# Softmax sums of four units in six: column blocks summed on VectorE and joined by a small product, in place of a product with ones

## The chip, the core and the metric

The kernel runs on one core of one Trainium2 chip. The metric is the time of one execution on the device in microseconds (us); a version's time is the median of its runs. The engines are TensorE (PE, with its weight loads shown apart as PEld), VectorE (DVE), ScalarE (ACT), GpSimd (POOL) and SyncE (SP), which issues most transfers. [...]

## The reference

Input x is 8 images of 384 channels and 32x32 pixels in float32. Four layers follow one another, each as x = x + layer(groupnorm(x)). Layer 0 is an attention with depthwise convolutions ahead of its projections, layer 1 a mixture of four experts, layer 2 a quantized depthwise and pointwise convolution, and layer 3 a deformable attention. Only layer 3's attention is touched:

```
q  = einsum(x, q_w)                       # 6 heads of 64 channels, 1024 queries
kv = einsum(x_s, kv_w)                    # x_s: 256 sampled positions
attn = softmax(q . k * 64**-0.5)          # over the 256 keys
out  = proj_w . (attn . v) + proj_b
```

The softmax needs, for each head and each query, the sum of 256 exponentials.

## The kernel before

Layer 0 is computed for all images first, up to about 1630 us. Then the images go through layers 1 to 3 one behind the other: a generator `layers(b)` records layers 2 and 3 of image b, and between its steps the main loop records units of layer 1 of image b+1 (three products each: `hidden`, tile ph, or `result`, tile y) so that TensorE has work while others are waited for. Each `yield` of the generator states how much time TensorE is expected to have free; when the sum reaches `UNIT` (2.6), a unit of layer 1 is recorded. The instruction order on each engine is then set by a scheduler, which may move an instruction ahead of one that was recorded before it, and tiles come from pools whose buffers are used again in turn.

Layer 3's attention of an image is `attend`. It has six units: three pairs of heads (`pr`), each in two halves of 512 queries (`h`). The two heads of a pair lie side by side: in the columns of scores and exponentials (2 x 512), and in the two halves of 64 partitions of what comes out. A unit u is made so:

- `scores`: the products of keys with queries, for the two halves of the keys (kc = 0, 1), into two tiles s of 128 keys x 1024.
- `exps`: ACT takes the exponential of each, tiles p, in SBUF. They come from the pool `flat`, which has five buffers and also serves `p01` and, at the start of the next image's layer 1, the three tiles `o` that are loaded from HBM.
- POOL adds the two halves: p01 = p[0] + p[1], 128 partitions x 1024.
- `weigh`: values times exponentials, tile pav, 64 partitions for each head x 512 queries. PSUM's pool for pav (`ps_v`) has one bank.
- `sums` (L1899): a product of ones (128x64) with p01, for each head 512 columns, so that every one of the 64 partitions of a head holds the sums of its 512 queries (tile pss, from the pool `ps_f` of three banks, which ph and y also use).
- DVE transposes pav in 32x32 blocks into tu (L1935), and in `divide` pss in the same way into ts (L1907); in ts the sum of a query is the same along 32 columns, so one column of each block is enough: a reciprocal of 128x16 (L1909), a multiply of tu (L1910), and a transpose back into att (L1913).

A matrix product in float32 is made of two passes on TensorE. The products of `weigh` and `sums` for the two heads use the two halves of the array's columns.

The loop is shifted by one: in the round of unit u, the scores of unit u+1 are recorded ahead of `weigh` for unit u, and the sums and the division are those of unit u-1 (`due3`). The last unit's sums and division follow the loop, then the projection (tile pf).

The reciprocals are also kept in `rec3`; at the end of the program their range is looked at, and if one is out of range, layer 3 is done again in a general way.

Of the kernel before, what the change touches and what calls it, by code (L numbers as in the profile page):

```python
# [7 lines left out]
F32 = mybir.dt.float32  # L8
AF = mybir.ActivationFunctionType
ALU = mybir.AluOpType  # L10
AX = mybir.AxisListType

B, C, H, W = 8, 384, 32, 32
N = H * W
P = 128
# [20 lines left out]
NPAIR3, HS, LS, NG = 3, 16, 256, 3  # L36
# [19 lines left out]
def tile_kernel(ctx: ExitStack, tc: tile.TileContext, i: dict, out: bass.AP):  # L56
    nc = tc.nc
# [3 lines left out]
    small = ctx.enter_context(tc.tile_pool(name="small", bufs=2))  # L61
# [205 lines left out]
    with ExitStack() as pa:  # L267
# [254 lines left out]
        for n, (u, kind, s) in enumerate(work):  # L522
            k, h = divmod(u, 2)
# [29 lines left out]
            if kind == "v":  # L553
                h, c = h + s, 0
# [5 lines left out]
            for p in passes:  # L560
                j, x = p
                c0, c1 = max(0, 1 - x), W - max(0, x - 1)
                for q in range(nq):
# [3 lines left out]
                    elif kind == "y":  # L567
                        g, j, w = s, q, slice(0, 64)
# [4 lines left out]
                    for r, rs in enumerate(quads):  # L573
                        nc.tensor.matmul(  # L574
                            banks[r][cols[q]].rearrange("p (h w) -> p h w", w=W)[:, :, c0:c1],
                            lhsT=cws[rs, c, 2 * h + g, x, w],
                            rhs=src[rs, :, c0 + x - 1 : c1 + x - 1],
                            start=(p == passes[0]), stop=(p == passes[-1]),
# [13 lines left out]
            for q in range(4):  # L592
                rows = quads[q]
                if kind == "y":
                    v, j = divmod(q, 2)
# [5 lines left out]
                else:  # L601
                    g, j = divmod(q, 2)
# [69 lines left out]
    with ExitStack() as pb:  # L672
# [252 lines left out]
        for k in range(2):  # L925
            qs = slice(k * HALF // 2, (k + 1) * HALF // 2)
            for m in range(KC):
                for c in range(KC):
                    nc.tensor.matmul(
                        pos[m][:, qs], lhsT=wo0[:, c, m * P : (m + 1) * P],  # L930
                        rhs=atts[B - 1][:, c, HALF:][:, qs], start=(c == 0), stop=(c == KC - 1),
# [24 lines left out]
    _, sco, sho = sc_o  # L956
# [51 lines left out]
    with tc.If(redo > 0):  # L1008
        with ExitStack() as pb:
# [5 lines left out]
            for v, nm in enumerate(("wq0", "wk0", "wv0")):  # L1015
                t = wb.tile(list(i[nm].shape), F32, name=f"{nm}_e")
# [6 lines left out]
            with tc.For_i(0, B) as bi:  # L1023
# [11 lines left out]
                for t in range(NT8):  # L1035
                    pv = bank(f"pv_e{t}")
                    for c in range(KC):
                        nc.tensor.matmul(
                            pv[:, :C], lhsT=act[2][:, c, t * P : (t + 1) * P],
                            rhs=w_in[2][:, c, :], start=(c == 0), stop=(c == KC - 1),  # L1040
# [8 lines left out]
                for v in range(2):  # L1049
                    ts = qp.tile([P, NPAIR0, N], F32, tag=f"qk{v}", name=f"qk{v}_e")  # L1050
                    for pr in range(KC):
                        for h in range(2):
                            pq = bank(f"pq{v}_e{pr}_{h}")
                            for c in range(KC):
                                nc.tensor.matmul(
                                    pq, lhsT=w_in[v][:, c, pr * P : (pr + 1) * P],
                                    rhs=rows_of(act[v][:, c, :], h * H // 2, (h + 1) * H // 2) if v == 0
                                    else act[v][:, c, h * HALF : (h + 1) * HALF],
                                    start=(c == 0), stop=(c == KC - 1),
# [8 lines left out]
                for pr in range(NPAIR0):  # L1068
                    qt, kt = qks[0][:, pr, :], qks[1][:, pr, :]
                    for h in range(2):  # L1070
                        pav = bank(f"pav_e{pr}_{h}")
                        for j, r in enumerate(HR):
                            hd = 2 * pr + j
                            pt = qp.tile([P, NT8, HALF], F32, tag="pt", name=f"pt_e{pr}_{h}_{j}")
                            for qc in range(4):
# [3 lines left out]
                                for kh in range(2):  # L1079
# [3 lines left out]
                                        start=True, stop=True,  # L1083
# [3 lines left out]
                                p = pp.tile([P, N], F32, tag="p", name=f"p{nm}")  # L1087
# [14 lines left out]
                            for kc in range(NT8):  # L1102
                                nc.tensor.matmul(
                                    pav[64 * j : 64 * j + 64, :],
                                    lhsT=vt[:, kc, 2 * hd : 2 * hd + 2, :].rearrange(
                                        "p a b -> p (a b)"
                                    ),
                                    rhs=pt[:, kc, :],
# [38 lines left out]
    def load_w(name):  # L1147
        src = i[name]
        t = wd.tile(list(src.shape), F32, tag=name, name=name + "_sb")
        nc.sync.dma_start(out=t, in_=src)  # L1150
        return t
# [237 lines left out]

    x2_dram = dram.tile([B, P, KC, N], F32, name="x2")  # L1390
    om_dram = dram.tile([B, 3, NG * LS], F32, name="omd")
    NU3 = 2 * NPAIR3
    rec3 = wd.tile([P, B * NU3, 16], F32, name="rec3")
    bad3 = wd.tile([P, 1], mybir.dt.int32, name="bad3")

# [428 lines left out]
    def attend(pl, b, xt, put, general, q, xs, fill=nothing):  # L1824
# [69 lines left out]
        if not general:  # L1894
            def sums(u, p01):

                pss = fbank(f"pss3_{b}_{u}")
                for j in range(2):
                    nc.tensor.matmul(  # L1899
                        pss[64 * j : 64 * j + 64, :], lhsT=ones[:, :64],  # L1900
                        rhs=p01[:, j * HALF : (j + 1) * HALF], start=True, stop=True,
                    )
                return pss

            def divide(pss, pr, h, u, tu):
                tss = pl.one([P, 16, 32], "ts", f"ts_{b}_{u}")
                nc.vector.transpose(tss.rearrange("p a b -> p (a b)"), pss)  # L1907
                rc = rec3[:, b * NU3 + u, :]
                nc.vector.reciprocal(rc, tss[:, :, 0])  # L1909
                nc.vector.tensor_tensor(  # L1910
                    tu, tu, rc.unsqueeze(2).to_broadcast([P, 16, 32]), ALU.mult
                )
                nc.vector.transpose(  # L1913
                    att[:, pr, h * HALF : (h + 1) * HALF], tu.rearrange("p a b -> p (a b)")
                )


            ps, due3 = exps(0, scores(*units[0])), None
            fill(1)
            yield UNIT  # L1920
            for u, (pr, h) in enumerate(units):
                p01 = pl.flat([P, N], f"p01_{b}_{u}")
                nc.gpsimd.tensor_tensor(p01, ps[0], ps[1], ALU.add)  # L1923
                nxt = scores(*units[u + 1]) if u + 1 < NU3 else None
                if last and nxt:
                    nxt = exps(u + 1, nxt)
                pav = weigh(pr, h, ps)
                if due3:
                    pss = sums(due3[2], due3[4])
                if nxt:  # L1930
                    ps = nxt if last else exps(u + 1, nxt)

                tu = pl.one([P, NG * LS], f"om{u % 2}", f"tu_{b}_{u}")[:, :HALF]
                tu = tu.rearrange("p (a b) -> p a b", b=32)
                nc.vector.transpose(tu.rearrange("p a b -> p (a b)"), pav)  # L1935
                if due3:
                    divide(pss, *due3[:4])
                due3 = pr, h, u, tu, p01
                if u < KC:
                    fill(1)  # L1940
                yield UNIT
                yield 0.0
            divide(sums(due3[2], due3[4]), *due3[:4])
            yield 3.0
        else:
            for pr, h in units:
                pav = vbank(f"pav3_{b}_{pr}_{h}")
                for j in range(2):
                    r = slice(64 * j, 64 * j + 64)
                    nm = f"3_{b}_{pr}_{h}_{j}"  # L1950
                    s = big(f"s{nm}").rearrange("p (a k) -> p a k", a=4)
                    for qc in range(4):
                        q0 = h * HALF + qc * P
                        nc.tensor.matmul(
                            s[:, qc, :], lhsT=q[r, pr, q0 : q0 + P], rhs=kt[r, pr, :],
                            start=True, stop=True,
                        )
                    mx = small.tile([P, 4], F32, tag="mx4", name=f"mx{nm}")
                    nc.vector.reduce_max(mx, s, AX.X, negate=True)
                    nc.vector.tensor_scalar(mx, mx, 0.125, None, ALU.mult)  # L1960
                    p = pl.flat([P, 4, LS], f"p{nm}")
                    rs = small.tile([P, 4], F32, tag="rs4", name=f"rs{nm}")
                    for qc in range(4):
                        nc.scalar.activation(
                            p[:, qc, :], s[:, qc, :], AF.Exp, bias=mx[:, qc : qc + 1],
                            scale=0.125, accum_out=rs[:, qc : qc + 1],
                        )
                    nc.vector.reciprocal(rs, rs)
                    nc.vector.tensor_tensor(
                        p, p, rs.unsqueeze(2).to_broadcast([P, 4, LS]), ALU.mult  # L1970
                    )
                    pt = pl.flat([P, 2, HALF], f"pt{nm}")
                    for kc in range(2):
                        tp = fbank(f"tp{nm}_{kc}")
                        for qc in range(4):
                            nc.tensor.transpose(
                                tp[:, qc * P : (qc + 1) * P], p[:, qc, kc * P : (kc + 1) * P], ident
                            )
                        nc.vector.tensor_copy(pt[:, kc, :], tp)
                    hd = 2 * pr + j  # L1980
                    for kc in range(2):
                        nc.tensor.matmul(
                            pav[r, :], lhsT=vt[:, kc, hd * 64 : (hd + 1) * 64], rhs=pt[:, kc, :],
                            start=(kc == 0), stop=(kc == 1),
                        )
                nc.vector.tensor_copy(att[:, pr, h * HALF : (h + 1) * HALF], pav)
# [140 lines left out]
    for b in range(1, B):  # L2127
        logits(b)
        del fetched[b, 0]
        for n in (2, 3) if b == 1 else (b + 2,):  # L2130
            if n < B:
                fetch_next(n)
        if b + 3 == B:
            w2, b2 = load_w("w2"), load_w("b2")
            wq3, wk3, wv3, wp3 = (load_w(n) for n in ("wq3", "wk3", "wv3", "wp3"))
            pb3, dw3, bn3, pw3 = (load_w(n) for n in ("pb3", "dw3", "bn3", "pw3"))
            ref3, npos, half3 = load_w("ref3"), load_w("npos"), load_w("half3")
        if b + 1 < B:
            for _ in range(3 if b < 6 else 2):
                units.pop(0)()  # L2140
# [81 lines left out]
def _layouts(a):  # L2222
# [3 lines left out]
    L = {}  # L2226
    L["x"] = a["x"].reshape(B, C, N)
    L["ident"] = np.eye(P, dtype=f)
    part4 = np.arange(P) // (GN_C // KC)
    L["g4"] = (part4[:, None] == part4[None, :]).astype(f) / f(GN_C // KC)  # L2230

    by3 = np.arange(C).reshape(P, KC).T.reshape(-1)
# [115 lines left out]
```

## Time and profile before

| what | value |
| --- | --- |
| median of 3 runs | 3465.93 us (3464.11 to 3468.15) |
| the profiled execution's own time | 3463.13 us |
| its span | 3461.3 us |
| PE busy | 3366.8 us (97%) |
| DVE busy | 1705.9 us (49%) |
| ACT busy | 1302.4 us (38%) |
| POOL busy | 204.4 us (6%) |
| sums on PE (L1899) | 192 passes of 128x512, in the six images' and the last two images' units |
| transposes of the sums on DVE (L1907) | 48, 0.708 us in the mean |

The profile is that of one execution. Its span begins with the first and ends with the last instruction; the execution's own time has 1.8 us more. A group's line gives the source line, the engine, the operation, output and input tiles by name, the count and the mean time. L820 and the like are lines of the kernel before; in the changed kernel the same code stands further down. A matrix product's record lasts longer than the time it occupies the array, since such records overlap; the chain that ended last shows the time by which one moves the next.

### The profile page before, as it was taken

To read this page: it belongs to the slowest core of one execution; us is meant where nothing else is said; L and a number is where in the kernel's file an instruction comes from. 1 tells how busy PE (TensorE), PEld (TensorE's weight loads), DVE (VectorE), ACT (ScalarE), POOL (GpSimd) and SP (SyncE) were. 2 spreads that over 40 slices of the span, in tenths; PEclk is the share of its full clock that TensorE was granted. 3 is DMA by queue.
4 is the path that set the end of the run, shared out by engine and by line. 5 is a ranking of instruction groups with operands and counts; after the bars stand their busy time and mean duration, and the time that the engine had idled before them with its cause. 6 is when DMAs were issued, how large, how long until landed. Compare 5 with 4: busy or idle time off the path is not lost.

```text
span 3461.3 us, 44963 instructions
## 1 busy us (share of the span) xinstructions
PE 3366.8 (97%) x18599; PEld 1445.9 (42%) x18599; DVE 1705.9 (49%) x2925; ACT 1302.4 (38%) x1519; POOL 204.4 (6%) x238
## 2 busy tenths in 40 slices
PE   6999999999999999998999999999999999999989
PEld 2433434343434343443344444444444444444443
DVE  8942232323232323234266475564754647548764
ACT  5655444444444444433222323223232232322341
POOL 2100000000000000000000100101001010010121
PEclk9999999999999999999999999999999999999999
DMA  9973121212121212022600010101101011010000
GB/s 360 299 207 80 27 80 27 80 27 80 27 80 27 80 27 80 27 80 84 267 25 19 35 57 20 53 22 36 47 28 55 22 36 40 35 55 22 0 19 38
DMA packets 86259, 234.01 MB, mean 68 GB/s; under 512 B 21672, under 2 KB 21896, under 8 KB 79130
## 3 DMA queue, kind: packets, MB, share of 16 engines
q1 hardware_dynamic: 83882, 222.75, 20.1%
q10 hardware_dynamic: 1248, 4.72, 0.4%
q8 instruction: 150, 2.46, 0.3%
q0 software_dynamic: 912, 3.53, 0.3%
q14 instruction: 67, 0.55, 0.1%
HBM read 145.77 MB, written 75.59 MB: 64 GB/s over the span
## 4 chain that ended last, share of the span: by engine, by line
PE 42%; DVE 7%; DMA 1%; ACT 1%; POOL 1%; issue 0%; DVEq 0%; ACTq 0%; POOLq 0%; SPq 0%
PE y L1504 12%; PE ph L1483 10%; DVE y L1625 4%; PE pq L1666 3%; PE pf L1992 3%; PE pw L1637 3%; PE s L1860 2%; PE pav L1886 2%; PE pk L1831 1%; DVE hd L1469 1%; DMA o<-o 1%; DVE off L1762 1%; PE pss L1899 1%; PE pv L1842 1%; PE xsb L1812 1%; PE pw_last L2041 1%
## 5 line engine op out<-in xcount | busy, mean ns | idle before, releaser
L827 ACT ACTIVATE p<-s 128x1024 f32<-128x1024 f32 x512 | 496.3, 1021 | 365.7 <-PE s L820 365.5
L835 PE MATMUL pav<-p,vt 64*64 64x512 f32 x4096 | 494.8, 588 | 0.0
L1483 PE MATMUL ph<-h,w_sb 128*128 128x512 f32 x1104 | 487.4, 595 | 6.0 <-ACT h L1432 4.6
L1504 PE MATMUL y<-hd,w_sb 128*128 128x512 f32 x1080 | 487.0, 599 | 3.5 <-DVE hd L1469 3.5
L820 PE MATMUL s<-qk,qk 48*64 48x512 f32 x2944 | 355.3, 592 | 0.0
L1483 PEld LDWEIGHTS ph<-h,w_sb 128*128 128x128 f32 x1104 | 206.8, 190 | 266.1 <-issue 248.1
L1504 PEld LDWEIGHTS y<-hd,w_sb 128*128 128x128 f32 x1080 | 199.7, 191 | 248.3 <-issue 233.8
L835 PEld LDWEIGHTS pav<-p,vt 64*64 64x64 f32 x4096 | 168.6, 133 | 273.3 <-issue 273.1
L796 DVE COPY ta<-pav 128x512 f32<-128x512 f32 (+1 forms) x65 | 44.2, 682 | 475.6 <-PE pav L835 475.6
L1493 ACT ACTIVATE hd<-ph,b_sb 128x512 f32<-128x512 f32 x180 | 122.7, 682 | 307.7 <-PE ph L1483 307.7
L1762 DVE SCALAR_TENSOR_TENSOR off<-q,dw_sb,off 128x225 f32<-128x225 f32 (+4 forms) x441 | 215.3, 541 | 2.6
L574 PE MATMUL pk<-xs,cws_sb 32*32 32x496 f32 (+3 forms) x3840 | 177.3, 600 | 40.0 <-POOL xs L402 30.8
L1625 DVE SCALAR_TENSOR_TENSOR y<-h,tap,y 128x961 f32<-128x961 f32 (+1 forms) x168 | 202.5, 1225 | 0.5
L820 PEld LDWEIGHTS s<-qk,qk 48*64 48x64 f32 x2944 | 109.6, 133 | 211.0 <-issue 190.1
L1877 ACT ACTIVATE p<-s 128x1024 f32<-128x1024 f32 x96 | 96.3, 1022 | 188.0 <-PE s L1860 156.7
L81 DVE COPY qk<-pq 128x512 f32<-128x512 f32 x46 | 31.8, 691 | 252.0 <-PE pq L258 252.0
L1469 DVE TENSOR_TENSOR hd<-hd,cb 128x512 f32<-128x512 f32 x180 | 122.0, 683 | 37.7 <-ACT hd L1493 37.5
L1923 POOL TENSOR_TENSOR p<-p,p 128x1024 f32<-128x1024 f32 x48 | 113.6, 2367 | 354.9 <-ACT p L1877 334.6
L574 PEld LDWEIGHTS pk<-xs,cws_sb 32*32 32x32 f32 (+1 forms) x3840 | 75.9, 111 | 139.7 <-issue 57.3
L820 PE MATMUL s<-ql,ql 48*64 48x512 f32 x1024 | 128.3, 592 | 0.2 <-ACT p L827 0.2
L1992 PE MATMUL pf<-att,wp_sb 128*128 128x512 f32 x288 | 127.9, 598 | 0.0
L711 PE MATMUL pv<-wv_sb,g 128*128 128x384 f32 x384 | 127.1, 489 | 0.0
(368 smaller groups left out, 3728.5 us busy)
## 6 DMA issues: line engine op xcount, KB each, us to landing
rqk<-y SPq DMA_DIRECT2D x96, 256.0 KB
g<-rqk SPq DMA_DIRECT2D x96, 256.0 KB
xs<-in_xs_dram SPq DMA_DIRECT2D x56, 384.0 KB
g<-rv SPq DMA_DIRECT2D x48, 256.0 KB
xh<-in_x_dram SPq DMA_DIRECT2D x48, 256.0 KB
f<-in_x_dram SPq DMA_DIRECT2D x24, 512.0 KB
f<-o SPq DMA_DIRECT2D x24, 512.0 KB
o<-ot SPq DMA_DIRECT2D x42, 256.0 KB
```

Of the source, the lines that this page charges most:

```text
L574: nc.tensor.matmul(banks[r][cols[q]].rearrange("p (h w) -> p h w", w=W)[:, :, c0:c1], lhsT=cws[rs, c, 2 * h + g, x, w], rhs=src[rs, :, c0 ...
L711: nc.tensor.matmul(pv[:, :C], lhsT=acts[b][2][:, c, t * P : (t + 1) * P], rhs=w_in[2][:, c, :], start=(c == 0), stop=(c == KC - 1),)
L820: nc.tensor.matmul(s[64 * k : 64 * k + 64, j * HALF : (j + 1) * HALF], lhsT=kt[r, k0 : k0 + 64], rhs=qt[r, h * HALF : (h + 1) * HALF], sta ...
L827: nc.scalar.activation(p, s, AF.Exp, scale=scale)
L835: nc.tensor.matmul(pav[k][64 * j : 64 * j + 64, :], lhsT=vts[b % 2][r, kc, 2 * hd : 2 * hd + 2, :].rearrange("p a b -> p (a b)"), rhs=p[r, ...
L1469: nc.vector.tensor_tensor(hd, hd, state["cb"], ALU.mult)
L1483: nc.tensor.matmul(ph, lhsT=w1[:, e, c, dc * P : (dc + 1) * P], rhs=state["h1"][c], start=(c == 0), stop=(c == KC - 1),)
L1493: nc.scalar.activation(hd, ph, AF.Relu, bias=b1[:, k : k + 1])
L1504: nc.tensor.matmul(y, lhsT=w2[:, e, dc, m * P : (m + 1) * P], rhs=state[h, k], start=(k == 0), stop=(k == NE * KC - 1),)
L1625: nc.vector.scalar_tensor_tensor(d, f, tap2[:, c, t : t + 1], d, ALU.mult, ALU.add)
L1762: nc.vector.scalar_tensor_tensor(d, f, dw3[:, t : t + 1], d, ALU.mult, ALU.add)
L1992: nc.tensor.matmul(pf[:, hs], lhsT=wp3[:, pr, m * P : (m + 1) * P], rhs=att[:, pr, hs], start=(pr == 0), stop=(pr == NPAIR3 - 1),)
```

## The change

For images 0 to 5 (`b < B - 2`), units 0 to 3 get their sums in another way. As soon as DVE has finished its part for the round, `block_sums` transposes p01 in 32x32 blocks (128x1024, into a tile `tp` of the buffer `ts`, which grows from 16x32 to 32x32 elements a partition) and sums each block's 32 columns: `bsum`, 128 partitions x 32. Partition 32i+r of column a then has the sum over the 32 keys of partition block i for query 32a+r (columns 0 to 15 for one head, 16 to 31 for the other). `join` adds the four partition blocks up: a product of `same` (128x64; entry 1 where row and column agree modulo 32, else 0) with 16 columns of bsum for each head. The result stands in the layout that `divide` wants, so the reciprocal reads it from PSUM and the transpose ts falls away. Units 4 and 5, and images 6 and 7, keep `sums`. `same` is a new input, loaded behind half3.

The order of instructions on the engines moves with it. On DVE the block transpose and the sum of unit u stand ahead of the transpose tu of unit u, or between the steps of the division of unit u-2. On TensorE one of the two products of unit 4's pss now stands ahead of pav of unit 5; both stood behind it. The `flat` buffers go round differently: the exponential of the second half of the keys no longer waits for a product pav of the unit before, and POOL's add of unit u+1 waits for the block transpose of unit u.

```diff
--- before.py
+++ after.py
@@ -1389,7 +1389,7 @@
 
     x2_dram = dram.tile([B, P, KC, N], F32, name="x2")
     om_dram = dram.tile([B, 3, NG * LS], F32, name="omd")
-    NU3 = 2 * NPAIR3
+    NU3, NB3 = 2 * NPAIR3, 4
     rec3 = wd.tile([P, B * NU3, 16], F32, name="rec3")
     bad3 = wd.tile([P, 1], mybir.dt.int32, name="bad3")
 
@@ -1902,11 +1902,34 @@
                     )
                 return pss
 
+            blocks = NB3 if b < B - 2 else 0
+
+            def block_sums(u, p01):
+
+                t = pl.one([P, 32, 32], "ts", f"tp_{b}_{u}")
+                nc.vector.transpose(t.rearrange("p a b -> p (a b)"), p01)
+                bsum = small.tile([P, 32], F32, tag="bsum", name=f"bsum_{b}_{u}")
+                nc.vector.reduce_sum(bsum, t, AX.X)
+                return bsum
+
+            def join(u, bsum):
+
+                pss = fbank(f"pbs3_{b}_{u}")
+                for j in range(2):
+                    nc.tensor.matmul(
+                        pss[64 * j : 64 * j + 64, :16], lhsT=same,
+                        rhs=bsum[:, 16 * j : 16 * j + 16], start=True, stop=True,
+                    )
+                return pss
+
             def divide(pss, pr, h, u, tu):
-                tss = pl.one([P, 16, 32], "ts", f"ts_{b}_{u}")
-                nc.vector.transpose(tss.rearrange("p a b -> p (a b)"), pss)
                 rc = rec3[:, b * NU3 + u, :]
-                nc.vector.reciprocal(rc, tss[:, :, 0])
+                if u < blocks:
+                    nc.vector.reciprocal(rc, pss[:, :16])
+                else:
+                    tss = pl.one([P, 16, 32], "ts", f"ts_{b}_{u}")
+                    nc.vector.transpose(tss.rearrange("p a b -> p (a b)"), pss)
+                    nc.vector.reciprocal(rc, tss[:, :, 0])
                 nc.vector.tensor_tensor(
                     tu, tu, rc.unsqueeze(2).to_broadcast([P, 16, 32]), ALU.mult
                 )
@@ -1926,7 +1949,7 @@
                     nxt = exps(u + 1, nxt)
                 pav = weigh(pr, h, ps)
                 if due3:
-                    pss = sums(due3[2], due3[4])
+                    pss = (join if due3[2] < blocks else sums)(due3[2], due3[4])
                 if nxt:
                     ps = nxt if last else exps(u + 1, nxt)
 
@@ -1935,7 +1958,7 @@
                 nc.vector.transpose(tu.rearrange("p a b -> p (a b)"), pav)
                 if due3:
                     divide(pss, *due3[:4])
-                due3 = pr, h, u, tu, p01
+                due3 = pr, h, u, tu, block_sums(u, p01) if u < blocks else p01
                 if u < KC:
                     fill(1)
                 yield UNIT
@@ -2134,7 +2157,7 @@
             w2, b2 = load_w("w2"), load_w("b2")
             wq3, wk3, wv3, wp3 = (load_w(n) for n in ("wq3", "wk3", "wv3", "wp3"))
             pb3, dw3, bn3, pw3 = (load_w(n) for n in ("pb3", "dw3", "bn3", "pw3"))
-            ref3, npos, half3 = load_w("ref3"), load_w("npos"), load_w("half3")
+            ref3, npos, half3, same = (load_w(n) for n in ("ref3", "npos", "half3", "same"))
         if b + 1 < B:
             for _ in range(3 if b < 6 else 2):
                 units.pop(0)()
@@ -2227,6 +2250,7 @@
     L["x"] = a["x"].reshape(B, C, N)
     L["ident"] = np.eye(P, dtype=f)
     part4 = np.arange(P) // (GN_C // KC)
+    L["same"] = np.tile(np.eye(32, dtype=f), (4, 2))
     L["g4"] = (part4[:, None] == part4[None, :]).astype(f) / f(GN_C // KC)
 
     by3 = np.arange(C).reshape(P, KC).T.reshape(-1)
```

## The prediction

> **What bounds the kernel now.** I read the page first, then the busy time by stretches, the chain that ended last, PE's waits, and the timeline of one unit of layer 3's attention. The page, and the stretch of 219 us that holds image 1's attention (columns: stretch, length, then busy time of PE, PEld, DVE, ACT, POOL, granted clock, DMA share, GB/s):
>
> ```profile
> span 3461.3 us, 44963 instructions
> ...
> PE 3366.8 (97%) x18599; PEld 1445.9 (42%) x18599; DVE 1705.9 (49%) x2925; ACT 1302.4 (38%) x1519; POOL 204.4 (6%) x238
> ```
> ```profile
> 2183.00:2402.00 219.00, 218.40 (x632) 98.17 (x631) 128.94 (x195) 62.79 (x84) 19.84 (x17) 1.00 0.10 37
> ```
>
> PE is full, at full clock; DVE has 90 us to spare. The chain through image 1's attention (start, length, what):
>
> ```profile
> 2187.40 1.87 PE pav L1886 x8
> 2189.26 0.86 PE pss L1899 x4
> 2190.12 2.77 PE y L1504 x6
> 2192.90 1.92 PE s L1860 x8
> 2194.81 1.87 PE pav L1886 x8
> 2196.68 0.86 PE pss L1899 x4
> ...
> 2209.64 1.03 PE pav L1886 x4
> ...
> 2210.76 1.03 ACT p L1877
> ...
> 2211.86 2.37 POOL p L1923
> ...
> 2214.24 4.42 DMA o<-o
> ```
>
> A unit is 7.42 us of PE without a gap, of which the sums (pss) take 0.86. At the image's end the chain leaves PE: unit 5's exponential, the POOL add, the load of o, then DVE and ACT, until the next image's first ph. PE's waits between 1960 and 3120 us (total, times, longest) say what that costs:
>
> ```profile
> PE ph L1483 <- ACT h L1432: 4.6, 5, 1.4
> ```
>
> The timeline gives it as 1.20, 0.38, 1.33, 0, 1.42 and 0.29 us for images 0 to 5. DVE's part of one unit, with POOL's add:
>
> ```profile
> 2189.38 0.72 DVE L1935 STREAM_TRANSPOSE tu<-pav 128x512 f32<-128x512 f32 x1 [5.84 <-PE pav L1886]
> 2189.61 2.35 POOL L1923 TENSOR_TENSOR p<-p,p 128x1024 f32<-128x1024 f32 x1 [5.11 <-ACT p L1877]
> ...
> 2190.17 0.72 DVE L1907 STREAM_TRANSPOSE ts<-pss 128x512 f32<-128x512 f32 x1
> 2190.92 0.25 DVE L1909 RECIPROCAL rec<-ts 128x16 f32<-128x16 f32 x1
> 2191.21 1.30 DVE L1910 TENSOR_TENSOR tu<-tu,rec 128x512 f32<-128x512 f32 x1
> 2192.54 0.71 DVE L1913 STREAM_TRANSPOSE att<-tu 128x512 f32<-128x512 f32 x1
> ```
>
> The multiply takes 1.30 us where one away from POOL's adds takes 0.69; the transposes aren't slowed.
>
> **What the Trainium skill says.** *TensorEngine Tiling (Array Packing)*, Key Properties: tiles load and multiply in parallel, and a change of tiling mode drains the array. The trace agrees: four passes of pss, two per column half, take 0.86 us where one pass alone takes 0.43, and y after pss takes 2.77 instead of 2.58. *SBUF — State Buffer*, Who interferes with whom: a DVE instruction with two SBUF inputs contends with POOL's reads, one with a single input doesn't, `tensor_reduce` never. That fits the 1.30; bn_stats (0.695 under an add) agrees for one input. The reduction under an add is not in this trace.
>
> **PE, the steady part.** Each of units 0 to 3 loses pss: 4 passes, 0.86 us. It gets the join: two products of 16 columns, each two passes in this type, with 64-column weights `same`, in the same two column halves as pav before it; so the mode change still falls once, ahead of y. No 16-column product is in the trace. The nearest rows of the chain have 128-column weights and 2 or 64 columns moved:
>
> ```profile
> 1857.21 0.12 PE gna_d L117 x2
> ...
> 1933.90 0.22 PE xs L1812 x2
> ```
>
> So a short pass costs 0.06 to 0.11 us. If the halves run side by side, two steps of 0.055 (half the weights of xs): 0.11. If they don't, four of 0.11: 0.44. *TensorE: Matmul & The Clock Gate*, LDWEIGHTS, prices a load by columns, columns/1.2 ns: 53 ns for 64, which speaks for the low end. I take 0.22: a saving of 0.64 a unit, bounds 0.42 and 0.75.
>
> **DVE.** A unit loses ts (0.72). It gains a transpose of 128x1024 (rows of 64, 256 and 512 columns take 0.245, 0.418, 0.711, so some 1.14 ns a column: 1.30) and a reduction of 1024 (L948: 1.22, taken as 1.25). The reciprocal from PSUM stays at 0.25. Net +1.83 a unit, 44 us in 24 units, inside 90 us of slack per image. It matters only through PE's waits: pav has one PSUM bank, so pav of unit u+1 waits for tu of unit u, and DVE is strictly in order. In the changed program's order the block transposes stand early: tp0, x, bsum0, bn, tu0, tp1, bsum1, tu1, rec0, tp2, multiply0, bsum2, att0, tu2, rec1, tp3 and so on. Each tp waits for POOL's add, and holds up the tu behind it.
>
> I walk through it with t=0 at unit 0's scores (2174.16), PE by the chain's lengths. pav0 6.6–8.5, pav1 13.2–15.0, join0 after it, pav2 20.0–21.9, pav3 26.9–28.8, pav4 33.75. POOL's add 0 is 4.6–6.95. tp0 to 8.3, x (0.75, ready since 4.7, its bank not needed before 15) to 9.05, bsum0 to 10.3, bn to 11.0, tu0 to 11.8: pav1 wants it at 13.2, 1.4 us spare. Add 1 now also waits for tp0 (one buffer for the sums): 8.3–10.65. tp1 to 13.1, bsum1 14.4, tu1 (after pav1) 15.8, wanted at 20.0. Exponential 2's second half no longer waits for pav1, so add 2 is 14.6–16.95; tp2 to 18.3, bsum2 20.3, tu2 22.7, wanted at 26.9. tp3, after add 3 (23.8), to 25.2, bsum3 27.1, tu3 29.6, wanted at 33.75. Joins want bsum 5 to 9 us after it is there. So PE never waits, and 3 units x 6 images x 0.64 = 11.5 us.
>
> **The tail of each image.** Unit 3's join lies behind pav4, where the chain has left PE, so I count from pav4's start. PE: join3 saves 0.64. But the new order puts one half of unit 4's pss ahead of pav5: alone in its column half, 2 x 0.43 = 0.86, part of it in a gap of 0.22 where pav5 waits today for tu4. That comes to zero: the first ph comes as far after pav4 as before. The chain: the second half of exponential 5 no longer waits for pav4, so add 5 ends at 3.76 instead of 4.65; the second load of o also needs half of pav5, so it goes out at 3.92 instead of 4.67, 0.75 earlier. What PE waits for falls by up to that: 0.75 + 0.38 + 0.75 + 0 + 0.75 + 0.29 = 2.9 us. Bounds: 0.86 lost and no chain moved, −1.3 (0.22 x 6), to +4.5 if all six gain 0.75.
>
> **Costed at nothing.** The load of `same` (32 KB): SP issues it at about 1701, between half3 and layer 2's raw weights, where issues stand up to 1.6 us apart; raw, x1 and what follows on that queue come that much later. DVE first reads raw at 1717.5, and the DMA engines fall idle at about 1710: 7 us of cover; beyond it DVE's routing queue would be late microsecond for microsecond. ACT does the same work. After the attention the order is that of before, and what follows starts from PE's work, so it moves along.
>
> **Sum.** 11.5 + 2.9 = 14.4 us off the profiled execution's 3463.1 (span 3461.3 and 1.8 around it): 3448.7. The median of the runs is 2.8 above that execution, so 3465.9 − 14.4 = 3451.5.
>
> **Rivals.**
> *The join costs nearly what it replaces* (0.10): drains and weight loads that don't overlap in tiled mode, some 0.2 a pass, 0.8 in all. Against it: gna's two passes at 0.12. It gives 18 x 0.06 and nothing at the tails: about 3465; between that and my bound of 0.44, within 0.2%.
> *The tail gives nothing* (0.12): pss4's lone half on PE, the loads bound by transfer (4.4 to 5.5 us in the chain) rather than by issue. 11.5 − 1.3 = 10.2: 3455.7.
> *DVE becomes the bound, slower* (0.06): tu behind tp and bsum. With both at twice my price (2.6 and 2.5), the walk puts tu0 at 14.2, pav1 1.0 late, and pav4 and pav5 about 2.5 late in all: 3.5 us an image against 2.4 gained, 6 x 1.1 = 7 us slower, 3473. It decides from about 4.5 us for the pair, against my 2.55. For it: one bank, strict order, 1.4 us spare at unit 0. Against it: both have one input, and rows of half the size.
> That the change doesn't do what it says I rule out for units 0 to 3: the 24 joins stand in PE's order in place of the sums.
>
> **How the numbers follow.** My forecast has 0.70 (3447 to 3456 with the bounds of join and tail), 0.02 is for a surprise of any sign. A change under 0.2% (7 us) can't be told from none here. Faster: 0.70 + 0.12 + 0.01 = 0.83; same: 0.10; slower: 0.07. The range, 3446 to 3460, holds my case and the tail's; the join's rival and the slower one are left out.
>
> **What would show it.** Right: no pss of units 0 to 3 in images 0 to 5, joins at 0.1 to 0.4 us in the chain, units of about 6.8 us, pav with no wait for tu, tp near 1.30 and bsum near 1.25, DVE some 44 us busier, PE's wait for ACT h under 4.6. Wrong: PE waits of pav on tu, joins above 0.5, y after a join longer than 2.77, a longer stall before ph.

## The result and the profile after

| | before | after |
| --- | --- | --- |
| median of 6 runs | 3465.26 us (3464.00 to 3468.41) | 3443.99 us (3440.91 to 3452.52) |
| ratio after to before, 95% interval | | 0.9941 (0.9928 to 0.9953) |
| profiled execution, its span | 3463.13, 3461.3 us | 3452.52, 3450.7 us |

The medians differ by 21.3 us; the ratio gives a gain of 0.59%, or 20.4 us. The forecast was 14.4 us (3451.5), and the measured time lies below the forecast's range of 3446 to 3460: the direction was right, the size too small.

The profiled execution after the change is the slowest of its six. It lost 8 us in the first 250 us, in layer 0, whose code is the same; the other executions of the kernels of this document scatter there too: the first scores of image 0 come at 1954.3 to 1962.7 us. So I compare stretches of the two traces from the first scores of an image on, and take totals from the medians.

The page after, engines' busy time, and the stretch of 216 us from behind weigh of unit 0 of image 1 to about the same place in image 2 (columns as in the prediction):

```profile
PE 3356.5 (97%) x18599; PEld 1449.0 (42%) x18599; DVE 1732.8 (50%) x2949; ACT 1300.2 (38%) x1519; POOL 204.4 (6%) x238
```
```profile
2187.50:2403.50 216.00, 215.82 (x632) 98.40 (x631) 133.43 (x200) 62.38 (x84) 19.95 (x17) 1.00 0.10 38
```

PE is as full as before, and an image is 3.5 us shorter, 215.9 instead of 219.3 from first scores to first scores on the mean. The chain through image 1's attention after the change (start, length, what):

```profile
2191.93 1.87 PE pav L1886 x8
2193.80 0.07 PE pbs L1919 x4
2193.87 2.77 PE y L1504 x6
2196.64 1.92 PE s L1860 x8
2198.56 1.87 PE pav L1886 x8
...
2213.69 0.07 PE pbs L1919 x4
2213.76 0.89 PE pss L1899 x2
2214.66 1.88 PE pav L1886 x8
2216.54 1.72 PE pss L1899 x6
2218.25 3.63 PE pf L2015 x8
2221.88 1.72 PE ph L1483 x4
```

A unit has 6.63 us instead of 7.42. The join (pbs) takes 0.07 to 0.08 us where pss took 0.86, and y behind it still takes 2.77. And the chain no longer leaves PE at the end of the image: ACT, POOL and the load of o are gone from it. PE's waits from 1960 to 3120 us say the same (total, times, longest); these are all above 0.15 us:

```profile
PE px L1726 <- DVE h L81: 1.1, 3, 0.6
PE pw L1637 <- DVE y L1625: 0.9, 5, 0.2
```

There is no wait of pav for tu, and the 4.6 us in which ph waited for ACT's h have gone, but for a gap of 0.12 us in image 5. On DVE, in image 1, the block transpose (tp) and the reduction (bsum) of unit 2 lie between the steps of unit 0's division:

```profile
2195.58 1.25 DVE L1910 STREAM_TRANSPOSE tp<-p 128x1024 f32<-128x1024 f32 x1 [0.88 <-POOL p L1946]
2196.75 0.65 DVE L1933 TENSOR_TENSOR tu<-tu,rec 128x512 f32<-128x512 f32 x1
2197.32 1.21 DVE L1912 TENSOR_REDUCE bsum<-tp 128x32 f32<-128x1024 f32 x1
2198.44 0.70 DVE L1936 STREAM_TRANSPOSE att<-tu 128x512 f32<-128x512 f32 x1
```

Measured from an image's first scores, TensorE passes these places (us; "third ph" is the first product after the place where ph waited before, and "norm" the first product of the next layer's group norm, gna_d):

| kernel | weigh of unit 4 | first ph | third ph, images 0 to 5 | norm, images 0 to 5 |
| --- | --- | --- | --- | --- |
| before | 35.41 | 45.38, in image 5 45.59 | 47.60, 46.78, 47.74, 46.35, 47.82, 47.00 | 61.55, 60.73, 61.69, 60.30, 61.77, 60.95 |
| after | 33.06 | 43.03 | 43.89 five times, 44.17 | 57.62 four times, 57.73, 58.12 |

Up to weigh 4 each image gains 2.35 = 3 x 0.784 us, 14.1 us in six images. From there to the norm the gains are 1.58, 0.76, 1.72, 0.33, 1.69 and 0.48: 6.6 us. Together 20.7 us, which is the gain of the medians but for 0.6.

### The profile page after: what moved, and what is told of

Same layout as the page of the kernel before. It is cut to its first block, busy times and chain, and to the rows that moved or that the text cites. A ratio compares the mean times of both kernels' runs of the same rounds, so it can differ in the third digit from the quotient of the medians.

```text
span 3450.7 us, 45025 instructions
## 1 busy us (share of the span) xinstructions
PE 3356.5 (97%) x18599; PEld 1449.0 (42%) x18599; DVE 1732.8 (50%) x2949; ACT 1300.2 (38%) x1519; POOL 204.4 (6%) x238
## 3 DMA queue, kind: packets, MB, share of 16 engines
q1 hardware_dynamic: 84026, 222.78, 20.1%
## 4 chain that ended last, share of the span: by engine, by line
PE 44%; DVE 7%; ACT 1%; POOL 0%; DMA 0%; issue 0%; DVEq 0%; POOLq 0%; ACTq 0%; SPq 0%
PE y L1504 12%; PE ph L1483 10%; DVE y L1625 4%; PE pf L2015 4%; PE pq L1666 3%; PE pw L1637 3%; PE pav L1886 3%; PE s L1860 2%; PE pk L1831 1%; DVE hd L1469 1%; DVE off L1762 1%; PE pv L1842 1%; PE plog L1231 1%; PE pss L1899 1%; PE xsb L1812 1%; PE pw_last L2064 1%
```

## The experiments

Gains are against the runs of the kernel before on the same chip (medians 3466.1 to 3466.7 us), worked out from the ratio: one minus the ratio, times 3466. What the expectations call the second ph is the third product of the table above, the one ahead of which TensorE waited for h.

**Unit 3 alone, and units 0 to 2 alone.** My theory after the result: two gains that add up, one a unit in the steady part, one in the tail that comes from unit 3 alone, because the second exponential of unit 5 takes the buffer of unit 3's p01. The rival: the tail gains because the loads of o have moved forward with everything else.

```diff
-            blocks = NB3 if b < B - 2 else 0
+            blocks = (NB3 - 1,) if b < B - 2 else ()
-                if u < blocks:
+                if u in blocks:
...
```

The other two places that ask for a unit below `blocks` change in the same way.

> The changed kernel with unit 3 alone summed in blocks of 32; units 0, 1 and 2 (and 4, 5) are summed by TensorE as before. Theory: two gains add up, 18 x 0.784 us in the steady units and some 6.5 us in the tails; the tail's part comes from unit 3 alone, since its p01 is the buffer that unit 5's second exponential waits for. Then TensorE runs as before up to weigh 4 of each image (35.41 us after the first scores), the second ph of each image starts at about 45.5 to 46.3 us after them (before: 46.4 to 47.8), and the gain is about 6.5 us: 3458.8. Rival: the tail gains because its loads of o start 2.35 us earlier against the other transfers: then this kernel gains nothing in the tail (within 1 us of before, 3464 to 3466).

Measured: 3461.60 us, ratio 0.9986 (0.9979 to 0.9993), a gain of 4.9 us (2.4 to 7.3). Weigh 4 stands at 35.41 as before, and the third ph at 46.46 in every image: no wait for h is left, though 46.46 is a little later than the 45.5 to 46.3 expected. The first ph is 0.22 us later than before (45.61), because pav of unit 5 now waits for DVE; PE's waits, 1960 to 3120 us:

```profile
PE pav L1886 <- DVE rec L1928: 1.0, 6, 0.2
```

The other half is NB3 = 3:

```diff
-    NU3, NB3 = 2 * NPAIR3, 4
+    NU3, NB3 = 2 * NPAIR3, 3
```

> The changed kernel with NB3 = 3: units 0, 1 and 2 in blocks, unit 3 summed by TensorE again. Theory: the three steady units keep 3 x 0.784 = 2.35 us an image (weigh 4 at 33.06 us), the tail is that of before, with TensorE's wait for h back (second ph some 11 to 12.4 us after weigh 4): 14.1 us gained, 3451.2. Rival, that the tail gains by the shift of its loads against other transfers: the tail is as short as in the changed kernel (second ph 10.8 us after weigh 4), and the time is that of the changed kernel, 3444 to 3446.

Measured: 3452.51 us, ratio 0.9956 (0.9940 to 0.9973), a gain of 15.3 us (9.4 to 20.8). Weigh 4 stands at 33.06, and the tail has its wait back, and the load of o in its chain (waits first, then the chain of image 1):

```profile
PE ph L1483 <- ACT h L1432: 6.2, 6, 1.9
```
```profile
2211.90 2.37 POOL p L1946
2214.27 0.02 issue
2214.28 5.58 DMA o<-o
```

The gains agree with a sum, 4.9 and 15.3 against 20.4 for the whole change, but their intervals are wide, so the places in the traces decide. Unit 3 alone ends the wait for h with weigh 4 where it was; units 0 to 2 shift everything by 2.35 us and keep the wait. The tail's gain is unit 3's, and the rival falls.

**The join's price.**

```diff
-                for j in range(2):
+                for j in [0, 1] * 4:
```

> The changed kernel with each join's two products issued four times over into the same bank. Theory: a join of 16 columns costs TensorE 0.075 us whole, so three more cost 0.225 us a unit: 18 x 0.225 = 4.1 us in the steady units and up to 6 x 0.225 = 1.4 us in the tails, 3448 to 3449.5, and weigh 4 comes 33.06 + 0.68 = 33.74 us after the first scores. Rival: a part of the join's cost is hidden at its place behind other work and only shows when it is repeated, 0.22 us each as the prediction took it: 18 x 0.66 = 11.9 us and more, 3456 to 3460.

Measured: 3453.45 us, ratio 0.9956 (0.9942 to 0.9970), a gain of 15.3 us (10.4 to 20.1): 5 us of the whole change's 20.4 are lost. The chain has, in each unit of image 1:

```profile
2193.82 0.42 PE pbs L1919 x16
2194.24 2.77 PE y L1504 x6
```

Sixteen passes take 0.42 us and four take 0.07, so each further set of four costs 0.117: more than the 0.075 of the theory, and far from the 0.22 of the rival. Weigh 4 comes at 34.11, 9 x 0.117 later, and the tail takes unit 3's repeats in without delay (6.43 us from weigh 4 to the first pf in both kernels). The records of the passes show how. In every set the two column halves start 6 to 7 ns apart, so they do work side by side, and from one pair of passes to the next it is 58 ns. Only from the first pair of a join to its second it is 28 ns; in image 1 the first pair's weights were loaded 0.43 us ahead. A single join has this short step alone, and repeating it adds six of the long ones: 0.35 us. The page *TensorE: Matmul & The Clock Gate* of the Trainium skill, in LDWEIGHTS, prices a weight load at its columns/1.2 ns, by which I estimate 53 ns for 64 columns; that is near the step of 58 ns with the two loads side by side. (The records of the loads last 137 ns each, but overlap.)

**VectorE's work without its use.** Units 0 to 3 take their sums from TensorE as before, the block sums are computed besides and not used.

```diff
-                    pss = (join if due3[2] < blocks else sums)(due3[2], due3[4])
+                    pss = sums(due3[2], due3[4])
-                due3 = pr, h, u, tu, block_sums(u, p01) if u < blocks else p01
+                if u < blocks:
+                    block_sums(u, p01)
+                due3 = pr, h, u, tu, p01
...
```

`divide` transposes pss in all units again.

> The changed kernel in which units 0 to 3 still take their sums from TensorE (the product with ones, the turn of its result, the reciprocal, as before), and VectorE's turn and reduction of p01 are done besides, their result unused. Theory: VectorE's 2.45 us a unit are covered, and unit 3's p01 is free only after TensorE's product has read it, as before, so that neither the steady units nor the tails change: within 2 us of before, 3463 to 3467. Rival, that VectorE is near its bound: its 2.45 us more (0.62 more than the change adds) delay tu or the exponentials' buffers, and the time is 5 us or more above before.

Measured: 3466.68 us, ratio 1.0001 (0.9993 to 1.0010), between 2.4 us gained and 3.5 lost. 24 x 2.45 = 59 us more on DVE cost nothing that can be told from this. In the trace pav of unit 5 waits 0.2 to 0.3 us for tu in each image, 1.7 us in all, and ph waits 1.4 us for h instead of 4.6. Why this execution's second loads of o were short (4.5 us on the mean) with the issue times of before, I can't say; it is one of the reasons for the repeated runs below.

**VectorE's margin.**

```diff
-                nc.vector.transpose(t.rearrange("p a b -> p (a b)"), p01)
+                for _ in range(2):
+                    nc.vector.transpose(t.rearrange("p a b -> p (a b)"), p01)
-                nc.vector.reduce_sum(bsum, t, AX.X)
+                for _ in range(2):
+                    nc.vector.reduce_sum(bsum, t, AX.X)
```

> The changed kernel in which VectorE turns and reduces each p01 of units 0 to 3 twice, with the same result: 4.9 us a unit instead of 2.45. Theory (the prediction's walk, in which a weigh product waits for tu once the pair passes some 4.5 us): 0.4 us of wait a unit in the steady part, up to 2.4 us once an image in the tail, where the run of unit 3 alone showed a wait of 0.2 us for VectorE already: weigh 4 at 33.1 to 34.7 us after the first scores, and 14 to 24 us more than the changed kernel, 3458 to 3468. Rival, that VectorE is far from bounding: the time of the changed kernel, 3444 to 3446.

Measured: 3448.18 us, ratio 0.9948 (0.9932 to 0.9965), a gain of 18.0 us, 2.4 below the whole change. PE's waits name the place:

```profile
PE pav L1886 <- DVE tu L1960: 2.4, 6, 0.4
```

Once an image, ahead of pav of unit 1, where I had found the least room, and nowhere else; weigh 4 moves by 0.47 us. What holds pav up is DVE's order: tu of unit 0 in image 1 begins only behind the doubled work, 4.3 us after pav of unit 0 has ended (at 2181.62):

```profile
2185.94 0.70 DVE L1960 STREAM_TRANSPOSE tu<-pav 128x512 f32<-128x512 f32 x1
```

The time is far below the 3458 to 3468 us expected. So the sign of the theory is right and its size wrong: the room at unit 0 was 2.45 − 0.40 = 2.05 us rather than 1.4, and in the units behind it no pav waits for DVE any more.

**Why the load of o became shorter.** With the records of landings I split the wait of the second addition of o into the issue of the second load and its length. In the kernel before the second load goes out 4.67 us after weigh 4, the third at 5.10, and in the changed kernel at 4.00 and 4.86: the second load 0.67 us earlier, and the third 0.86 instead of 0.43 us behind it. The load itself also lasted less, 4.18 us on the mean of images 0 to 4 instead of 4.93. To try whether the third load's distance does that, the kernel before gets one edit: two buffers are passed over, each with a load of 32 bytes, so that the third load of o waits for a later release. It then goes out at 6.53, and the second at 4.67 as before. (The loads at the end of image 5 are left as they were.) The two small loads are the edit's only other work.

```diff
-            ots = [pl.flat([P, N], f"o{b}_{c}") for c in range(KC)]
+            ots = []
             for c in range(KC):
+                if c == KC - 1 and 0 < b < B - 1:
+                    for i in range(2):
+                        skip = pl.flat([P, N], f"skip{b}_{i}")
+                        nc.sync.dma_start(out=skip[0:1, 0:8], in_=o_dram[b, 0:1, c, 0:8])
+                ots.append(pl.flat([P, N], f"o{b}_{c}"))
                 nc.sync.dma_start(out=ots[c], in_=o_dram[b, :, c, :])
```

> The kernel before with one edit: two buffers of the rotation are passed over (each takes a few bytes by a small load) ahead of the third load of o, so that this load waits for the p01 of unit 5 and starts about 1.3 us after the second instead of 0.43. All sums are TensorE's. Theory: the second load of o lasts longer in the kernel before (4.05 to 5.46 us from issue to landing, mean 4.9) than in the changed kernel (4.05 to 4.83, mean 4.3) because the third starts 0.43 us behind it instead of 0.86 and shares its way: then its mean falls to 4.3 or less here, and the second ph starts up to 1 us earlier. Rival: the length of the second load hangs on the first, or on other traffic: it stays at 4.9 on the mean, and the second ph at 46.4 to 47.8.

In this execution the second load took 4.45 us, not the 4.3 or less expected, and the gain in time is not clear of noise (ratio 0.9993, 0.9984 to 1.0002). So the kernel before and this one were run three times more, in turn:

> The kernel before once more, unchanged, for a second look at its loads of o. If the second load's length follows from the third's start 0.43 us behind it, its mean over images 0 to 4 is 4.7 us or more again (first look 4.92); if it was chance in one execution, it is 4.0 to 4.5, as in the changed kernel.

> The kernel before with the third load of o delayed, once more, for a second look. If the third load's place sets the second's length, the mean over images 0 to 4 is 4.5 us or less again (first look 4.45) and at least 0.3 us below that of the kernel before beside it; if it was chance, the two kernels do not differ.

> The kernel before, a third look at its loads of o. If the third load's place sets the length of the second: a mean over images 0 to 4 of 4.7 us or more (so far 4.92 and 4.88). If chance: anything from 4.2 to 5.2.

> The kernel before with the third load of o delayed, a third look. If the third load's place sets the length of the second: a mean over images 0 to 4 of 4.5 us or less (so far 4.45 and 4.28), below the kernel before beside it. If chance: anything from 4.2 to 5.2.

> As the third look at the kernel before: 4.7 us or more if the third load's place sets the length of the second.

> As the third look at the kernel with the third load delayed: 4.5 us or less if the third load's place sets the length of the second.

Length of the second load from issue to last landing, mean of images 0 to 4, and PE's wait for h in all six images:

| pair of runs | third load 0.43 us behind (kernel before) | third load 1.87 us behind |
| --- | --- | --- |
| 1 | 4.93, wait 4.6 | 4.45, wait 2.7 |
| 2 | 4.88, wait 4.0 | 4.27, wait 1.3 |
| 3 | 4.71, wait 3.4 | 4.26, wait 1.0 |
| 4 | 4.87, wait 4.0 | 4.45, wait 2.1 |

In the chain of image 4, second pair of runs, kernel before first:

```profile
2874.62 5.62 DMA o<-o
```
```profile
2871.26 4.45 DMA o<-o
```

The two columns don't overlap: with the third load 1.87 us behind, the second is shorter by 0.49 us (4.85 to 4.36). Single loads of the kernel before spread from 4.00 to 5.63 us, those with the third delayed from 3.88 to 4.79. The other runs' traces point the same way, with one exception. Where the third load is 0.86 us behind, in the changed kernel, with unit 3 alone, with the fourfold join and with the doubled work on DVE, the second takes 4.07 to 4.28 us on the mean; with units 0 to 2 alone, 0.43 us behind, it takes 5.19. The exception is the run with block sums beside the sums, with 4.49 at the distance of before; that stays open.

How much the third load's distance does in the changed kernel isn't shown, as the test moved it to 1.87 us and not to 0.86. At 0.86 the second load is even shorter than at 1.87, so the distance can't be all. A rival that no run tried by itself is the first load: in the four runs at 0.86 it is also further ahead of the second, 1.99 to 2.21 us instead of 1.80. The runs with five or six units, further below, fit that: there the first is only 0.86 us ahead, and the second takes 4.38 to 4.55 though the third is 2.25 behind. The whole times of the single executions (3460.8 to 3468.7 us) scatter more than the 1 to 3 us that are at stake.

**More units and more images.** Where unit 3 in blocks pays, unit 4 might too.

```diff
-    NU3, NB3 = 2 * NPAIR3, 4
+    NU3, NB3 = 2 * NPAIR3, 5
```

> NB3 = 5: units 0 to 4 in blocks. Theory: 1.72 us of TensorE's sums turn into a join of 0.08 in the tail, but the second ph still waits for the load of o_1, which starts when p01 of unit 4 is free and has 0.6 us to spare in the changed kernel: 0.5 to 0.8 us an image gained, 3 to 5 us in all, 3439 to 3441. Rival: VectorE's turn and reduction of unit 4 stand ahead of the first addition of o in the tail and make tu 5, the att of the last units and the first ph late: 0 to 1.5 us an image lost, 3444 to 3453.

Measured: 3434.06 us (3431.08 to 3435.21), ratio 0.9908 (0.9891 to 0.9924), a gain of 31.9 us: some 10 us beyond the changed kernel, twice or more what I had expected (3 to 5). The chain of image 1's tail:

```profile
2201.68 1.87 PE pav L1886 x8
2203.55 0.19 PE pbs L1919 x8
2203.74 1.06 PE pf L2015 x2
2204.80 1.87 PE pav L1886 x8
2206.66 0.86 PE pss L1899 x4
2207.52 14.83 PE pf L2015 x34
2222.35 2.58 PE ph L1483 x6
```

In the changed kernel unit 4's sums cost PE not 0.86 but about 1.7 us: the lone half ahead of pav (0.89), and the other half in the six passes of pss (1.72, where unit 5's four take 0.86 here). Now a second join of 0.12 stands for them: about 1.6 us an image, 9.8 in six. The scheduler also puts all projections ahead of ph, so that neither the loads of o nor DVE are waited for. From one image's first scores to the next's it is 1.9 us less than in the changed kernel, 215.9 to 213.9 on the mean.

All six units (NB3 = 6, and the division behind the loop takes a join too):

> NB3 = 6 (the last division takes its sums from a join too): all six units in blocks. Theory: the last join waits for VectorE's turn and reduction of unit 5's p01 (2.45 us) where it had a product of 0.86, and the projection of its last third waits behind that: no gain over five units, 0 to 2 us an image lost against them, 3440 to 3452. Rival: other projections fill TensorE in the meantime, and another 0.8 us an image is gained: 3435 to 3437.

Measured: 3435.10 us, ratio 0.9911 (0.9894 to 0.9927): no gain over five. Images last 0.3 us longer (214.2), and PE's wait of pw for y is 2.8 us, where five units leave none above 0.15. That is what the theory expected.

Image 6 too (`b < B - 1`), and all images (`b < B`), both with five units:

> NB3 = 5, and image 6 in blocks too. Theory: image 6's attention is bound by TensorE as the others are, and gives back about 0.784 us a unit for three to five units: 2.4 to 3.9 us below five units on images 0 to 5 (3434.1), 3430 to 3432. Rival: image 6 runs beside the last image's work, where VectorE or other waits set the pace: no change, or up to 3 us lost, 3434 to 3437.

> NB3 = 5 in images 0 to 7. Theory: the last image, too, saves 0.784 us a unit where TensorE sets its pace: up to 3.9 us below the run with image 6, 3427 to 3431. Rival: the last image has no other work to fill TensorE, so that a join waits for VectorE's turn and reduction of 2.45 us in every unit: 1 to 8 us lost, 3431 to 3440.

Measured: 3435.57 us, ratio 0.9912 (0.9895 to 0.9928), and 3432.91 us, ratio 0.9907 (0.9890 to 0.9923). Neither can be told from five units in six images, as the rivals had it. Image 6 reaches its first projection 1.7 us later than with sums (71.85 instead of 70.20 us after its first scores), and PE waits for DVE there (image 6 and the last image, 3020 us to the end, run with image 6):

```profile
PE pav L1886 <- DVE tu L1958: 5.6, 2, 4.1
...
PE pav L1886 <- DVE rec L1928: 2.8, 1, 2.8
```

Of the first, 4.1 us stand in image 6, but with image 6 left to sums a wait of 5.4 us for tu stands there too; the wait for rec, also in image 6, is new.

Five units, six units and the two wider versions can't be told apart (3432.91 to 3435.57 us). The simplest of them is five units in images 0 to 5, 3434.06 us.

## Why the prediction was right in direction and wrong in size

- **PE bounds, and what leaves PE is time.** Right: PE has no gap in a unit before or after, and weigh 4 moves by exactly three savings.
- **The join, 0.22 us with bounds 0.11 and 0.44.** This term of the sum was mis-sized: 0.07 to 0.08 in place, 0.117 if repeated. I had worked out 0.11 for two halves side by side, had the Trainium skill's *TensorE: Matmul & The Clock Gate*, LDWEIGHTS, on that side, and took the middle of the two cases all the same. The saving is 0.784 a unit instead of 0.64, outside its own bound of 0.75: 18 x 0.144 = 2.6 us of the miss. The walk's times for pav of units 3 and 4 (26.9 and 33.75) don't follow from its own saving either, which gives 26.8 and 33.5; nothing hangs on that.
- **DVE.** The prices were right (1.20 to 1.25 for 1.30, 1.20 to 1.22 for 1.25), and so was "PE never waits" for the steady part. The six reductions that run under a POOL add take 1.204 to 1.206 us and the others 1.206 to 1.221, which agrees with what the prediction took from *SBUF — State Buffer*, Who interferes with whom, in the Trainium skill. DVE is 27 us busier, not 44. In units 0 and 1 the multiply no longer meets POOL's add and falls from 1.30 to 0.65; in units 2 and 3 it still does and takes 1.36 and 1.40. Together its 48 instructions take 7.4 us less, which the price had left out. The multiply isn't slowed evenly under the add: in all 40 cases of both traces it ends 0.55 us after the add does, after 1.30 to 2.78 us, as if it waited for the add's end. The lengths of all DVE instructions add up to 40 us more; busy time has 27, because it counts overlapping records once, such as the multiply at 2196.75 above, which begins before tp ends at 2196.83.
- **The tail on PE comes to zero up to the first ph.** Right to the hundredth in images 0 to 4: 9.97 us from weigh 4 to the first ph in both kernels. What it hid: the lone half of unit 4's sums, which the run with five units removes.
- **The tail's chain, 2.9 us.** This step failed. Its mechanism was right (unit 3's p01 frees the buffer for exponential 5, and add 5 ends at 3.73 where 3.76 was foreseen; the second load was to go out at 3.92 and went out at 4.00), and unit 3 alone shows it. But "falls by up to 0.75 each" took the load's length as fixed. The earlier issue alone, 0.67 us, would have ended 2.7 of the 4.6 us of waiting. But the load also became shorter, by some 0.7 us on the mean. The second load moved forward, and the third, which goes out as pav of unit 5 ends, did so by less (5.10 to 4.86); that the third load's distance can shorten the second is shown, by 0.5 us at 1.87, and what share it has here stays open. So the second addition of o starts 1.86, 1.02, 1.86, 0.57, 1.69 and 0.48 us earlier, and the 4.6 us of waiting go. The remaining 2.0 us of the 6.6 weren't in the sum at all: 0.2 to 0.4 us an image. In the kernel before the products behind the wait run slower: in image 1 two ph take 1.13 us, where two take 0.86 elsewhere in the chain. Why isn't shown, and image 3, which has no wait before, gains 0.33 too.
- **The load of `same` costs nothing.** Right: the first scores of image 0 come at 1957.3 us on the mean of the ten profiled executions with that load (1954.5 to 1962.7) and at 1957.3 on the mean of the eight without it (1954.3 to 1961.5); with this scatter, a cost of a microsecond or two would not be seen.
- **The rivals.** A dear join and a tail that gives nothing are refuted by the chain. The slower one, DVE as the bound, was rightly given little, but its price was wrong: at 4.9 us for the pair, an image loses 0.47 us up to weigh 4, where my walk made it 3.5 at 5.1 and the turning point 4.5. It is not a danger at this size.
- **The range.** It missed because the two terms that were off were off in the same direction, each beyond its own bound; that the load's length would go the same way as the join was not foreseen. 11.5 + 2.6 + 6.6 = 20.7 us.

## What to carry to other kernels

Where a wait is the end of a chain through several transfers, an earlier issue of one of them also changes its distance to the others: here the second of three 512 KB loads got shorter when the third came later, and the estimate that kept its length fixed was too low. A product that stood alone in one column half of a pair cost as much as the pair (0.89 us against 0.86), so look for such halves in the chain before pricing the removal of one. And where two derived cases and a measured range lie side by side, work out the sum at both ends before settling in the middle.

## What was not expected of the hardware

- Two products of 16 columns in the two column halves, four passes in float32, moved TensorE's chain by 0.07 to 0.08 us; twelve more passes added 0.35 us, or 58 ns for each pair of halves, whose passes start 6 to 7 ns apart.
- The second 512 KB load of o, with the first ahead of it and the third behind it on the same queue, took between 4.00 and 5.63 us from issue to landing in the same kernel, with the next load issued 0.43 us behind it, and 3.88 to 4.79 with the next 1.87 us behind.
- DVE's transpose of 128x1024 in float32 takes 1.20 to 1.25 us, and its reduction to 128x32 takes 1.204 to 1.206 under a POOL add and 1.206 to 1.221 without one (no transpose ran under an add).
- DVE's multiply of two SBUF inputs, begun under a POOL add, ended 0.55 us after the add in all 40 cases, and took 1.30 to 2.78 us; away from the adds it took 0.65 to 0.69.
